# The begin of the Gram stage: the constant row is made first, and two weight loads go behind the second step's transfers

## Chip, cores and metric

The kernel runs on one core of one Trainium2 chip. What counts is the time of one execution in device microseconds (us), as the median of several runs. All data is fp32. The engines are named as the profile names them: PE (TensorE, with its weight loads as PEld), DVE (VectorE), ACT (ScalarE), POOL (GpSimd) and SP (SyncE, which here only issues DMA transfers).

## The reference

Two bottleneck layers run one after the other on `x` of shape (64, 1024, 14, 14). Both have the same form, cut here to what matters:

```python
def layer(x, w1, g1, be1, w2, g2, be2, w3, g3, be3, residual_scale):
    out = relu(bn(conv1x1(x, w1), g1, be1))            # 1024 -> 256
    out = relu(bn(conv3x3(out, w2, pad=1), g2, be2))   # 256 -> 256
    out = bn(conv1x1(out, w3), g3, be3)                # 256 -> 1024
    out = softplus(residual_scale)[0] * out
    return relu(x + out)

def bn(x, gamma, beta):      # statistics of this batch
    mean, var = mean(x, axis=(0, 2, 3)), var(x, axis=(0, 2, 3))
    return gamma * (x - mean) * rsqrt(var + 1e-5) + beta
```

## The kernel before

**Stages.** The 64 x 196 = 12544 pixels (`NPX`) of all images are columns; channels are the 128 partitions (`P`). The 256 middle channels are two halves (`MS`), and all of them stay in SBUF as `y_all` [128, 2, 12544]. Per layer `b` the kernel does the first convolution, the 3x3 convolution (whose last stage is the `columns` matmuls), then a Gram stage, and then the third convolution with the residual sum, which for layer 0 is woven together with layer 1's first convolution.

**What the Gram stage is for.** The third batch norm needs mean and variance of a convolution that has not run yet. As that convolution is linear, both follow from the sums and the products of the 256 middle channels over all pixels. `gram` (line 1116) computes this matrix of products. It works through the pixels in 49 blocks of 256 columns (two groups of 128, `CH` = 2). For each block the channels have to be turned into columns and the pixels into partitions: a tile `zt` [128 pixels, 2, 256 channels + 2 columns of ones]. Six `zt` buffers are used in turn. TensorE then multiplies the block with itself, 8 matmuls for each block, into two accumulators, `upper` in the PSUM bank with the tag `cp` and `lower` in the bank `ap`. While it does so for one block, the next block's `zt` is being made.

**Two ways to make `zt`.** In the order of the code:

- Blocks 0 to 3 and 4 to 7 (the two pieces in `still`) are turned by TensorE: `by_tensor` does four transposes by matmul with the identity (line 1205) into a PSUM tile, and VectorE adds a constant row `c_row` while it copies the result into `zt` (line 1212).
- Blocks 8 to 48 (the seven pieces in `moved`: step 0 has five blocks, steps 1 to 6 have six each) are first rearranged by DMA. `move(k)` sends the 32x32 squares of step k into one of three buffers in turn, `homes[k % 3]`: for step 0 eight transfers of SP and eight of POOL with 80 KB each, for each later step seven of SP and five of POOL with 96 KB. The squares on the diagonal are copied by ScalarE (`stay(k)`). For the first layer one of the three buffers is the tile `ws`. `by_vector` (line 1221) is then a VectorE transpose of 32x32 squares.

Before a block can be used, `y_all` must be normalized in place: scale, shift and relu, by ScalarE (`norm`, recorded at the helper's line 338) or VectorE (`norm_vector`, lines 590 and 592). For accuracy a constant for each channel is subtracted too: on VectorE in place for the moved pieces (`less`, line 1163), and for the others by the `c_row` that is added after the transpose. `c_row` holds that constant as a row, the same in all partitions: `center_row` (line 1191) makes it with two matmuls of `minus_c` against the identity into a PSUM tile with the tag `ax`, and ScalarE copies it to SBUF.

**The order of the begin.** `pairs()` (line 1228) writes it out by hand: norms of the first two blocks, norms of the next two, `center_row`, and then the blocks, with norms, subtractions and moves in between; `n` counts the first eight blocks. `move(0)` is at n = 1, `move(1)` at n = 4, `move(2)` at n = 7, and each later `move` stands two steps ahead of its use. `keep_in_program_order` fixes the order of the instructions that it wraps on their engine; others may be placed by a scheduler, which also assigns the waits. `busy` (line 180) issues filler matmuls, identity against a broadcast column with 448 columns, whose results nobody reads: seven of them into the bank `m` at the end of the 3x3 convolution (line 1106), and one into `ax` after the transposes of block 0. A filler counts as two passes in the trace, as fp32 matmuls do.

**The weights.** The third convolution's weights `w3` (one transfer of 1 MB, `load_w3`, line 168) and, in layer 0, the next layer's `w1` (four transfers of 256 KB, `load_w1`, line 136) are issued on SP ahead of the Gram (lines 1649 and 1651). Their first readers stand near the end of the Gram: `combine_w3` after block 38 and `combine_w1` after block 44 (`beside`), which form weight sums on VectorE.

Of the kernel before, what the change touches and what calls it, by code (L numbers as in the profile page):

```python
# [38 lines left out]
FP = mybir.dt.float32  # L39
# [3 lines left out]
P = 128  # L43
N, C, H, W = 64, 1024, 14, 14
HW = H * W
M = 256
CS = C // P
MS = M // P
# [9 lines left out]
Q = P // 2  # L58
# [32 lines left out]
def bottlenecks(ctx: ExitStack, tc: tile.TileContext, x, w1s, w2s, w3s, pars, out):  # L91
    nc = tc.nc
# [40 lines left out]
            )  # L133
        return xt

    def load_w1(pool, b, queue):

        w = pool.tile([P, MS, 2, CS // 2, P], FP, tag="w1", name=f"w1_{b}")
        n = CS // 2
        for h, o in itertools.product(range(2), range(MS)):  # L140

            step = n // 2 if b == h == o == 0 else n
            for s in range(0, n, step):
                queue.dma_start(out=w[:, o, h, s : s + step], in_=w1s[b][:, o, h, s : s + step])
        return w

    def sums_tile(pool, n):

# [16 lines left out]
        n = CS // 2  # L165
        return combine([[w[:, k, o * n : (o + 1) * n] for k in range(MS)] for o in range(2)], s)

    def load_w3(pool, b):
        w = pool.tile([P, MS, CS, P], FP, tag="w3", name=f"w3_{b}")
        nc.sync.dma_start(out=w, in_=w3s[b])  # L170
        return w

    def matmul(*args, **kw):

        tc.keep_in_program_order(nc.tensor.matmul(*args, **kw))  # L175

    def busy(psum, tag, n, with_=None):

        v = ident if with_ is None else with_
        for i in range(n):  # L180
            matmul(psum.tile(448, tag), v, v[:, :1].to_broadcast([P, 448]), start=True, stop=True)

    def filters(pieces, spare):

# [409 lines left out]
    def conv2(b, par, aff, early, rest):  # L594
# [457 lines left out]
        psum, pool, stats = rest  # L1052
# [12 lines left out]
        l, m, l2 = first.bank("l"), second.bank("m"), second.bank("l")  # L1065
# [22 lines left out]
        queue = queue[1:] + list(itertools.islice(coming, 1))  # L1088
        for k in range(1, NG * NF):
# [13 lines left out]
            item.columns(*qs)  # L1103
            finished.send(item)
            queue = queue[1:] + list(itertools.islice(coming, k > 1))
        busy(psum, "m", 7)

    def conv3(psum, t, o, w3, tag=None):
        ps = psum.tile(tag=tag)
# [3 lines left out]
            )  # L1113
        return ps

    def gram(psum, pool, homes, aff, minus_c, beside):

        upper, lower = psum.tile(3 * Q + 1, "cp"), psum.tile(2 * Q + 2, "ap")  # L1120
        zts = [pool.tile([P, CH, M + 2], FP, tag=f"zt{i}", name=f"zt{i}") for i in range(NZT)]
        for zt in zts:
            nc.gpsimd.memset(zt[:, :, 0 : M + 2 : M + 1], 1.0)
# [32 lines left out]
        def normed(a, e, slots=both):  # L1156
            for s in slots:
                norm(s, y_all[:, s, a:e], aff, act)
# [31 lines left out]

        def center_row():

            ps = psum.tile(M, "ax")
            for s in range(MS):
                matmul(
                    ps[:, s * P : (s + 1) * P], minus_c[:, s : s + 1].to_broadcast([P, P]), ident, start=True, stop=True
                )
            act(c_row, ps, AF.Copy)
# [28 lines left out]

        def pairs():

            for a in 0, px:  # L1230
                norm_vector(1, y_all[:, 1, a : a + px], aff)
                normed(a, a + px, (0,))
            normed(2 * px, 4 * px, (0,))
            center_row()
            rest = [(piece, s) for piece in still for s in range(MS)]
            (second, end), half = still[1], sum(still[1]) // 2
            for n, a in enumerate(a for piece in still for a in range(*piece, px)):
                yield by_tensor(a)
                if n == 0:
                    busy(psum, "ax", 1)  # L1240
                    norm_vector(1, y_all[:, 1, 2 * px : 4 * px], aff)
                    normed(*moved[0])
                elif n == 1:
                    less(*moved[0])
                    move(0)
                    normed(second, end, (0,))
                    normed(second, half, (1,))
                elif n == 3:
                    norm_vector(1, y_all[:, 1, half:end], aff)
                    normed(*moved[1])  # L1250
                elif n == 4:
                    less(*moved[1])
                    move(1)
                    normed(*moved[2])
                elif n == 5:
                    less(*moved[2], both[:1])
                    stay(1)
                elif n == 6:
                    less(*moved[2], both[1:])
                    normed(*moved[3])  # L1260
                elif n == 7:
                    move(2)
                    stay(2)
            for k, (a, e) in enumerate(moved):
                for i in range((e - a) // px):
                    yield by_vector(k, i)
                    if i in (1, 3) and k and k + 2 < len(moved):
                        less(*moved[k + 2], both[i // 2 : i // 2 + 1])
                        if i == 3:
                            move(k + 2)  # L1270
                            if k + 3 < len(moved):
                                normed(*moved[k + 3])
                            stay(k + 2)
                    elif i in (0, 5) and k > 1 and rest:
                        piece, s = rest.pop(0)
                        less(*piece, (s,))
            assert not rest
# [315 lines left out]
    with tc.tile_pool(name="first", bufs=1) as one, tc.tile_pool(  # L1593
        name="first_x", bufs=2
    ) as x_left, ExitStack() as scope:
        xpools = x_right, x_left
        psum = Psum(scope, ["ps"], ps=4, ay=2)
        for i in range(1, 3):
            one.tile([P, CS // 2, PX], FP, tag=f"at{i}", name=f"at{i}")
        w1 = load_w1(one, 0, nc.scalar)  # L1600
        pair = [load_x(x_right, 0, t, CS if t == 0 else 2) for t in range(2)]
        for b in range(2):
            p = keep.tile([P, NPAR], FP, tag=f"par{b}", name=f"par{b}")
            nc.scalar.dma_start(out=p, in_=pars[b][:, :NPAR])
            par.append(p)
        sps = [softplus(p) for p in par]
        nc.scalar.activation(small.tile([P, 1], FP, tag="root", name="root"), sps[1], AF.Sqrt)
        masks.make_identity(nc, ident)
        busy(psum, "ps", 3, ones)
        w1 = combine_w1(w1, sums_tile(one, 1)[:, 0])  # L1610

        border = Border(0, stats1, x_scope)
        for t, xt in enumerate(pair):
            plain_conv1(psum, t, xt, w1[0], par[0], stats1)


        spare = [y_all[:, i, NPX - CS * PX :] for i in range(MS)]
        pieces = list(itertools.product(range(2), range(MS), range(MS)))
        work = filters(pieces, spare)
        total, calls, count = FSTEPS * len(pieces), 6 * (T // 2 - 1 - CS // MS), itertools.count(1)  # L1620

        def beside():
            i = next(count)
            for _ in itertools.islice(work, total * i // calls - total * (i - 1) // calls):
                pass

        def items():
            for t in range(2, T, 2):
                xs = [load_x(xpools[t // 2 % 2], 0, t + i) for i in range(2)]
                yield Conv1(psum, one, xs, (t, t + 1), w1, par[0], stats1, border)  # L1630

        for _ in stream(items(), T // 2 - 1, beside):
            pass

    for b in range(2):
# [9 lines left out]
        with tc.tile_pool(name=f"last_{b}", bufs=1) as one, tc.tile_pool(  # L1645
            name=f"last_x_{b}", bufs=2 if b == 0 else 5
        ) as x_left:
            xpools = (x_right, x_left) if b == 0 else (x_left, x_left)
            w3 = load_w3(one, b)
            if b == 0:  # L1650
                w1 = load_w1(one, b + 1, nc.sync)
            aff = affine(aggregate(stats2, 0), pb, G2, BE2)
            with ExitStack() as scope:
                if b == 0:
                    psum = Psum(scope, ["cy", "ay", "cx", "cy", "ay"], cy=2, ay=2)
                else:
                    psum = Psum(scope, ["cy", "cx"], cy=2, cx=2, cp=2)
                with tc.tile_pool(name=f"gram_{b}", bufs=1) as pool:
                    def x_tile(name, t=0):
                        return xpools[t].tile([P, CS * PX], FP, tag="x", name=name)  # L1660


                    ws = sums_tile(one, 2 - b)
                    homes = [x_tile("home"), x_tile("home") if b else ws.rearrange("p i n -> p (i n)"), x_tile("home", 1)]

                    made_c, made_a = [], []
                    beside = {NPX // (CH * P) - 10: lambda: made_c.append(combine_w3(w3, ws[:, 0]))}
                    if b == 0:
                        beside[NPX // (CH * P) - 4] = lambda: made_a.append(combine_w1(w1, ws[:, 1]))
                    grams = gram(psum, pool, homes, aff, minus_c, beside)  # L1670

                    made = [conv3(psum, 0, 0, w3, "cx" if b else "ay")]
                    mv3 = small.tile([P, CS, nc.vector.BN_AGGR_DIM], FP, tag="mv3", name="mv3")
                    conv3_stats(psum, pool, grams, w3, mv3, ("cy", "cp", "cy", "cp" if b else "cx"), homes[2])
# [59 lines left out]
```

## Time and profile before

Three runs took 1919.19, 1918.64 and 1917.91 us; the median is 1918.64 us.

| profiled execution | |
|---|---|
| its own time | 1919.69 us |
| span of its instructions | 1917.9 us |
| granted TensorE clock (1 is full speed) | 1.000 |
| 583 to 646 us (layer 0's Gram) | PE busy 62.48 of 63.00, DVE 54.84, ACT 45.42, DMA share 0.74, 221 GB/s |
| 1534 to 1598 us (layer 1's Gram) | PE busy 63.06 of 64.00, DVE 52.26, ACT 45.71, DMA share 0.69, 216 GB/s |
| 646 to 1534 us (between them) | PE busy 883.85 of 888.00, DVE 698.57, DMA share 0.52 |

How to read it: the busy time of an engine leaves out the instructions that only issue or wait, and the DMA share is the mean busy share of the 16 DMA engines. In lines of the timeline the first number is the start in us from the span's begin, the second the duration; an entry in square brackets is how long the engine had been idle before the instruction, and the last thing that it waited for. `out<-in` are the program's names of the tiles. In the chain of waits each line is a stretch of the path that ended last, with start and length; "issue" is a time in which the engine waited for nothing that the profile shows.

### The profile page before, as it was taken

Reading aid. Unit: us, or ns where it says so; the run is one execution under the profiler, and the core shown is the slowest. Engines: PE = TensorE matmul, PEld = TensorE weight load, DVE = VectorE, ACT = ScalarE, POOL = GpSimd, SP = SyncE. Lnnn points to the kernel's source line nnn. Section 1 sums busy time; section 2 is a strip of 40 time slices with the busy share of each in tenths; the row PEclk is TensorE's granted clock in tenths of the full one; section 3 lists DMA queues with packets and bytes.
Section 4 is the critical chain, followed back from the end, with each engine's and each line's share of the span. In section 5 each row is a group of like instructions: output and inputs, shape, how many; then the busy total and the mean of one; then the engine's idle time right before and its main releaser. Section 6 shows DMA issues by size and latency. Waiting matters only on the chain.

```text
span 1917.9 us, 28732 instructions
## 1 busy us (share of the span) xinstructions
PE 1901.9 (99%) x10236; PEld 1595.2 (83%) x10236; DVE 1543.6 (80%) x2491; ACT 1086.2 (57%) x2160; POOL 572.0 (30%) x682
## 2 busy tenths in 40 slices
PE   9999999999999999999999999999999999999999
PEld 5555557999998799999999999989999986555555
DVE  5787767999998867677767767789999986888786
ACT  2222214677778255555555555557777692666665
POOL 0111100211204133333434334302121141666664
PEclk9999999999999999999999999999999999999999
DMA  7777644887956534444444444359788466899898
GB/s 286 273 249 278 216 156 154 208 216 207 220 165 172 205 147 169 169 175 183 179 171 168 168 177 177 125 176 219 212 206 225 139 167 254 289 325 348 313 336 304
DMA packets 198527, 408.77 MB, mean 213 GB/s; under 512 B 37104, under 2 KB 175024, under 8 KB 181872
## 3 DMA queue, kind: packets, MB, share of 16 engines
q1 hardware_dynamic: 159712, 321.85, 49.1%
q0 software_dynamic: 33056, 34.03, 8.6%
q10 hardware_dynamic: 5616, 51.06, 6.4%
q8 instruction: 81, 1.33, 0.3%
q14 instruction: 62, 0.51, 0.1%
HBM read 263.75 MB, written 115.34 MB: 198 GB/s over the span
## 4 chain that ended last, share of the span: by engine, by line
PE 92%; DMA 2%; DVE 2%; ACT 2%; POOL 1%; issue 1%; SPq 0%; DVEq 0%; ACTq 0%; POOLq 0%
PE ay L175 17%; PE cy L175 17%; PE columns L175 14%; PE cp L175 11%; PE ap L175 10%; PE m L175 7%; PE l L175 6%; PE cx L175 5%; PE ax L175 4%; PE ps L175 1%; DMA x<-mid 1%; ACT y L338 1%; ACT home L338 1%; DMA home<-y 1%; POOL home L1184 0%
## 5 line engine op out<-in xcount | busy, mean ns | idle before, releaser
L338 ACT ACTIVATE cu<-cy,scale 128x196 f32<-128x196 f32 (+1 forms) x552 | 256.4, 473 | 280.2 <-PE cy L175 274.8
L175 PE MATMUL columns<-v,ub 128*128 128x224 f32 (+1 forms) x1536 | 302.3, 338 | 2.0 <-ACT columns L846 1.1
L338 ACT ACTIVATE x<-x,shift 128x392 f32<-128x392 f32 x452 | 255.0, 613 | 72.8 <-POOL x L530 53.6
L175 PEld LDWEIGHTS columns<-v,ub 128*128 128x128 f32 x1536 | 269.0, 188 | 7.5 <-ACT columns L846 2.2
L504 DVE SCALAR_TENSOR_TENSOR x<-cp,scale,x 128x196 f32<-128x196 f32 (+1 forms) x368 | 178.2, 484 | 98.8 <-PE cp L175 95.8
L175 PE MATMUL cy<-ct,ws 128*128 128x196 f32 (+1 forms) x736 | 221.8, 383 | 1.2 <-ACT cu L338 1.2
L175 PE MATMUL ay<-at,ws 128*128 128x196 f32 (+1 forms) x768 | 212.7, 382 | 0.0
L525 POOL TENSOR_TENSOR x<-x,cu 128x196 f32<-128x196 f32 (+1 forms) x184 | 160.0, 869 | 172.5 <-ACT cu L338 163.8
L530 POOL TENSOR_TENSOR x<-x,cu 128x392 f32<-128x392 f32 x124 | 125.9, 1015 | 191.5 <-DVE x L504 191.5
L175 PEld LDWEIGHTS ay<-at,ws 128*128 128x128 f32 x768 | 139.3, 190 | 34.5
L175 PEld LDWEIGHTS cy<-ct,ws 128*128 128x128 f32 x736 | 133.4, 190 | 36.4 <-ACT cu L338 3.7
L175 PE MATMUL l<-diffs,ub 128*128 128x224 f32 (+1 forms) x768 | 149.6, 337 | 0.3 <-ACT sd L1476 0.3
L551 POOL TENSOR_TENSOR x<-x,cu 128x392 f32<-128x392 f32 x120 | 121.9, 1017 | 87.2 <-DVE x L504 60.4
L175 PE MATMUL m<-sums,ua 128*128 128x224 f32 (+1 forms) x752 | 146.0, 336 | 0.2 <-DVE sums L667 0.2
L338 ACT ACTIVATE au<-ay 128x196 f32<-128x196 f32 (+1 forms) x140 | 53.4, 381 | 152.3 <-PE ay L175 149.6
L175 PEld LDWEIGHTS l<-diffs,ub 128*128 128x128 f32 x768 | 134.6, 189 | 1.4 <-ACT sd L1476 0.6
L504 DVE SCALAR_TENSOR_TENSOR x<-cx,scale,x 128x196 f32<-128x196 f32 (+1 forms) x184 | 89.1, 484 | 56.7 <-PE cx L175 56.7
L175 PEld LDWEIGHTS m<-sums,ua 128*128 128x128 f32 x752 | 131.4, 189 | 1.3 <-DVE sums L667 0.7
L175 PE MATMUL cy<-y,w 128*128 128x196 f32 (+1 forms) x408 | 125.3, 393 | 0.0
L175 PE MATMUL cx<-y,w 128*128 128x196 f32 (+1 forms) x400 | 122.6, 391 | 0.0
L175 PE MATMUL cp<-y,ws 128*128 128x196 f32 (+1 forms) x368 | 113.6, 390 | 1.9 <-DVE x L504 1.9
L175 PE MATMUL cy<-ct,w 128*128 128x196 f32 (+1 forms) x368 | 110.9, 383 | 0.5 <-ACT cu L338 0.5
(238 smaller groups left out, 3909.3 us busy)
## 6 DMA issues: line engine op xcount, KB each, us to landing
x<-in_x SPq DMA_DIRECT2D x62, 1568.0 KB, 6.8
ub<-u SPq DMA_DIRECT2D x92, 768.0 KB, 5.6
x<-mid SPq DMA_DIRECT2D x32, 1568.0 KB, 8.4
mid<-x ACTq DMA_DIRECT2D x31, 1568.0 KB, 5.1
out<-x SPq DMA_DIRECT2D x123, 392.0 KB, 5.7
ua<-u SPq DMA_DIRECT2D x92, 256.0 KB, 3.1
u<-y POOLq DMA_DIRECT2D x48, 256.0 KB, 5.5
home<-y SPq DMA_DIRECT2D x70, 96.0 KB, 3.6
```

The costliest lines, as they stand in the source:

```text
L175: tc.keep_in_program_order(nc.tensor.matmul(*args, **kw))
L338: tc.keep_in_program_order(nc.scalar.activation(*args, **kw))
L504: nc.vector.scalar_tensor_tensor(v, bank, self.scale[:, o : o + 1], v, ALU.mult, ALU.add)
L525: nc.gpsimd.tensor_add(self.part(1, 1), self.part(1, 1), u3)
L530: nc.gpsimd.tensor_add(v, v, self.u12)
L551: nc.gpsimd.tensor_add(v, v, self.u12[:, i * self.n : (i + 1) * self.n])
```

## The change

- `center_row` moves from behind the first norms to the head of `pairs()`. Its PSUM tile is no longer one of its own with the tag `ax`; it is the unused rest of an accumulator's bank, `cp` in layer 0 and `ap` in layer 1. Its ScalarE copy so stands ahead of the norms in ScalarE's order.
- The seven fillers into `m` at the end of the 3x3 convolution go. Behind the row's matmuls there are five (into the bank `ap` in layer 0, `ax` in layer 1) and one more into `ax`.
- The loads of `w3` and `w1` no longer stand ahead of the Gram. The tiles are allocated there, and `load()` issues the transfers, still on SP, at n = 4: behind SP's seven transfers of `move(1)` and ahead of `move(2)`. Their order is now fixed by hand. The first `w1` of the kernel, loaded at its begin on ScalarE's queue, keeps its place.
- The pool of the Gram stage gets `reuse_waits="tile"`, so that an allocation waits tile by tile for what held its memory before.

In the built programs nothing else moves: VectorE's and POOL's orders are the same.

```diff
-    def load_w1(pool, b, queue):
+    def w1_tile(pool, b):
+        return pool.tile([P, MS, 2, CS // 2, P], FP, tag="w1", name=f"w1_{b}")
+    def load_w1(w, b, queue):
...
-                queue.dma_start(out=w[:, o, h, s : s + step], in_=w1s[b][:, o, h, s : s + step])
-        return w
+                tc.keep_in_program_order(
+                    queue.dma_start(out=w[:, o, h, s : s + step], in_=w1s[b][:, o, h, s : s + step])
+                )
...
-            matmul(psum.tile(448, tag), v, v[:, :1].to_broadcast([P, 448]), start=True, stop=True)
+            matmul(psum.tile(448, tag) if isinstance(tag, str) else tag, v, v[:, :1].to_broadcast([P, 448]), start=True, stop=True)
...
             finished.send(item)
             queue = queue[1:] + list(itertools.islice(coming, k > 1))
-        busy(psum, "m", 7)
...
-        upper, lower = psum.tile(3 * Q + 1, "cp"), psum.tile(2 * Q + 2, "ap")
+        banks = psum.tile(512, "cp"), psum.tile(512, "ap")
+        upper, lower = banks[0][:, : 3 * Q + 1], banks[1][:, : 2 * Q + 2]
...
         def center_row():
-            ps = psum.tile(M, "ax")
+            ps = banks[b][:, M : 2 * M]
...
         def pairs():
+            center_row()
+            busy(psum, "ax" if b else banks[1][:, :448], 5)
+            busy(psum, "ax", 1)
             for a in 0, px:
                 norm_vector(1, y_all[:, 1, a : a + px], aff)
                 normed(a, a + px, (0,))
             normed(2 * px, 4 * px, (0,))
-            center_row()
...
                 elif n == 4:
                     less(*moved[1])
                     move(1)
+                    load()
                     normed(*moved[2])
...
-            w3 = load_w3(one, b)
+            w3 = w3_tile(one, b)
             if b == 0:
-                w1 = load_w1(one, b + 1, nc.sync)
+                w1 = w1_tile(one, b + 1)
...
-                with tc.tile_pool(name=f"gram_{b}", bufs=1) as pool:
+                with tc.tile_pool(name=f"gram_{b}", bufs=1, reuse_waits="tile") as pool:
...
+                    def load():
+                        tc.keep_in_program_order(nc.sync.dma_start(out=w3, in_=w3s[b]))
+                        if b == 0:
+                            load_w1(w1, b + 1, nc.sync)
+                    grams = gram(psum, pool, homes, aff, minus_c, b, load, beside)
```

More of the change, by code (lines that the diff above doesn't have):

```diff
@@ L134, in load_x @@
         return xt
-    def load_w1(pool, b, queue):
-        w = pool.tile([P, MS, 2, CS // 2, P], FP, tag="w1", name=f"w1_{b}")
+    def w1_tile(pool, b):
+        return pool.tile([P, MS, 2, CS // 2, P], FP, tag="w1", name=f"w1_{b}")
+    def load_w1(w, b, queue):
         n = CS // 2
@@ L166, in combine_w3, with w3_tile @@
         return combine([[w[:, k, o * n : (o + 1) * n] for k in range(MS)] for o in range(2)], s)
[L168 to L171, printed above, removed]
+    def w3_tile(pool, b):
+        return pool.tile([P, MS, CS, P], FP, tag="w3", name=f"w3_{b}")
     def matmul(*args, **kw):
@@ L1114, in conv3, with gram @@
         return ps
-    def gram(psum, pool, homes, aff, minus_c, beside):
-        upper, lower = psum.tile(3 * Q + 1, "cp"), psum.tile(2 * Q + 2, "ap")
+    def gram(psum, pool, homes, aff, minus_c, b, load, beside):
+        banks = psum.tile(512, "cp"), psum.tile(512, "ap")
+        upper, lower = banks[0][:, : 3 * Q + 1], banks[1][:, : 2 * Q + 2]
         zts = [pool.tile([P, CH, M + 2], FP, tag=f"zt{i}", name=f"zt{i}") for i in range(NZT)]
@@ L1599, in bottlenecks @@
             one.tile([P, CS // 2, PX], FP, tag=f"at{i}", name=f"at{i}")
-        w1 = load_w1(one, 0, nc.scalar)
+        w1 = w1_tile(one, 0)
+        load_w1(w1, 0, nc.scalar)
         pair = [load_x(x_right, 0, t, CS if t == 0 else 2) for t in range(2)]
@@ L1669, in bottlenecks @@
                         beside[NPX // (CH * P) - 4] = lambda: made_a.append(combine_w1(w1, ws[:, 1]))
-                    grams = gram(psum, pool, homes, aff, minus_c, beside)
+                    def load():
[3 more added lines that the diff above has]
+                    grams = gram(psum, pool, homes, aff, minus_c, b, load, beside)
                     made = [conv3(psum, 0, 0, w3, "cx" if b else "ay")]
```

## The prediction

> **What bounds the kernel now.** I read the page first, then the chain of waits around the two Grams (583 to 646 us and 1534 to 1598 us), then the timelines there, then the DMA windows.
>
> ```profile
> span 1917.9 us, 28732 instructions
> PE 1901.9 (99%) x10236; PEld 1595.2 (83%) x10236; DVE 1543.6 (80%) x2491; ACT 1086.2 (57%) x2160; POOL 572.0 (30%) x682
> ...
> PE 92%; DMA 2%; DVE 2%; ACT 2%; POOL 1%; issue 1%; SPq 0%; DVEq 0%; ACTq 0%; POOLq 0%
> ```
>
> TensorE sets the time: 99% busy, 92% of the chain. All that is left beside its work is 1917.9 - 1901.9 = 16 us of idle, so a change that removes no useful matmul can win only pieces of that. One piece stands at the begin of each Gram (chain of waits, start and length in us):
>
> ```profile
> 579.44 5.29 PE m L175 x14
> 584.73 0.37 PE ax L175 x4
> 585.10 0.19 ACT y L338
> 585.29 0.42 issue
> 585.71 0.37 ACT c_row L338
> 586.08 0.04 issue
> 586.12 1.02 PE ax L175 x2
> ```
>
> Seven filler matmuls (14 passes), then the constant row's two, then the chain leaves TensorE for 1.0 us: it goes over ScalarE's copy of `c_row`. The timeline says why:
>
> ```profile
> 584.01 1.80 ACT L338 ACTIVATE y<-y,shift,scale 128x256 f32<-128x256 f32 x3 [1.14 <-DVE shift L1508]
> ...
> 585.01 0.60 PE L1205 MATMUL cy<-ident,y 128*128 128x128 f32 x4
> ...
> 586.12 1.02 PE L175 MATMUL ax<-ident 128*128 128x448 f32 x2 [0.52 <-ACT c_row L338]
> 586.16 0.69 DVE L1212 TENSOR_TENSOR zt<-cy,c_row 128x512 f32<-128x512 f32 x1 [0.63 <-ACT c_row L338]
> ```
>
> The copy is queued behind three norms, though its input needs none of them. TensorE waits for it 0.52 us (its next filler reuses the bank that the copy reads), VectorE 0.63. The second Gram shows the same at 1537.59 (0.51) and 1537.62 (0.63).
>
> The second part of the change moves weights on SP's queue:
>
> ```profile
> 579.87 0.35 SPq L170 DMA_DIRECT2D w<-in_w  x1
> 580.27 2.08 SPq L144 DMA_DIRECT2D w<-in_w  x4
> 590.00 5.52 SPq L1184 DMA_DIRECT2D home<-y  x8
> 595.77 5.05 SPq L1184 DMA_DIRECT2D ws<-y  x7
> 600.93 12.74 SPq L1184 DMA_DIRECT2D home<-y  x14
> ```
>
> Now the weights go out ten microseconds ahead of `move(0)` (590.00) and have landed by 587.9; nothing waits for them until the combinations on VectorE at 631.75. Where they go, the queue is close packed. What they would meet there is visible where VectorE waits for transfers, and in the DMA share (last but one column; before it length, then busy us of PE, PEld, DVE, ACT and POOL, and the clock):
>
> ```profile
> 604.15 1.31 DVE L1221 STREAM_TRANSPOSE zt<-ws 128x512 f32<-128x512 f32 x2 [1.33 <-DMA ws<-y]
> ...
> 617.21 0.71 DVE L1221 STREAM_TRANSPOSE zt<-home 128x512 f32<-128x512 f32 x1 [0.76 <-DMA home<-y]
> ```
>
> ```profile
> 606.00:608.00 2.00, 2.00 (x34) 1.82 (x32) 2.00 (x4) 1.97 (x2) 0.00 (x0) 1.00 0.41 95
> 608.00:610.00 2.00, 2.00 (x34) 1.79 (x32) 2.00 (x4) 2.00 (x3) 1.18 (x3) 1.00 0.33 76
> ```
>
> **The row ahead of the norms.** In the built order `center_row` stands right behind the last `columns` matmul; its wait is for a VectorE result from before 576, so it starts at 579.3. Then come 5 + 1 fillers instead of 7. Row 0.44 us (584.57 to 585.01) plus 12 passes of 0.378 (5.29 / 14) gives 579.28 + 0.44 + 4.54 = 584.26: TensorE is ready 0.75 us earlier than at 585.01, and idles until the norms. ScalarE's copy (0.36) falls into its wait of 1.14 us before 584.01, between `sd` (ends 582.87) and the first norm: hidden at no cost, and if that cover were gone the norms would be 0.27 later (585.71 to 585.98). The transposes need ScalarE's first norm (584.01 + 0.60 = 584.61) and VectorE's first pair (584.58 + 0.29 = 584.87). I add 0.08 for the handover, so the second transpose starts at 584.95; three of them (0.45) bring the filler to 585.40 instead of 586.12: **0.72 us** gained. Bounds: 0.52 (only the wait goes) and 0.75. VectorE's first sum can start at 585.5 instead of 586.16, behind its second norm pair (ends 585.53): 0.66. The dropped filler (0.76) is worth nothing by itself; TensorE waits for norms in its place.
>
> Does the lead last through blocks 0 to 12? I took, block by block, the time between the end of VectorE's `zt` and TensorE's first weight load on it: 0.17 us at block 7, 0.23 at block 8, else 0.35 or more. These `zt` move with TensorE's transposes and with `less`, whose norms on ScalarE come 0.27 earlier with slack behind them; `move(0)` goes at 589.4. So the lead holds to within 0.05. The pool's waits by tile release memsets that already stand behind POOL's statistics (until 581.4): nothing.
>
> **The weights, first Gram.** `load()` stands behind `move(1)`'s seven SP transfers and ahead of `move(2)`'s. SP issues w3 at 600.93 - 0.72 + 0.1 = 600.3, w1's four pieces until 602.8 (0.35 + 2.08 and gaps), then `move(2)`: 2.5 - 0.72 = 1.8 us later than now. SP allows eight transfers in flight: in the built order each waits for the landing of the one eight places before. So the fourth to seventh transfer of `move(2)` now wait for w3 and for three pieces of w1. POOL's five of `move(2)` and of `move(3)` are queued elsewhere but use the same engines.
>
> The 2.1 MB took 5.0 us of all DMA engines (share 0.84 of 582 to 588). Behind `move(1)` (lands 604.0 - 0.7 = 603.3) and beside POOL's half until 605, I put w3's landing at 606.5, the pieces of w1 0.63 apart, the third at 608.4; the last transfer of `move(2)` then takes 0.6 for its issue and 2.2 (the shortest landing of the group): **611.2** instead of 608.9 now. Below: 609.8, if the idle share around 606 to 610 takes most of it. Above: 613.2, all 5.0 us added to 608.2.
>
> The Trainium skill (DMA: Bandwidth & Descriptors, "Issuing engines are not separate DMA queues") says that transfers of all issuers end on the same 16 engines and interleave; taken alone it speaks against this change and gives the 613.2, which would make the sum about 2 us worse. The windows above show 0.59 x 2 + 0.67 x 2 = 2.5 us of engine time free in 606 to 610; 613.2 - 2.5 = 610.7 is near my value.
>
> What is late next? VectorE transposes `move(2)`'s first block now at 609.60, long after the landing, and `move(3)`'s at 617.21 after 0.76 of waiting; 617.21 - 0.76 - 609.60 = 6.85 us is its own work between, in order, `less` for later steps included. In that stretch TensorE's smallest margin is 0.82 (block 27). With TensorE 0.72 earlier 0.10 is left, so the first block has to start by 617.31 - 6.85 = 610.46. It starts at 611.2 + 0.15: 0.9 late, and TensorE gives that back. First Gram: -0.72 + 0.9 = **+0.2** (bounds -0.72 and +2.2).
>
> **The weights, second Gram.** Only w3, one transfer. Here VectorE is the tight engine:
>
> ```profile
> 1556.91 1.30 DVE L1221 STREAM_TRANSPOSE zt<-home 128x512 f32<-128x512 f32 x2 [2.96 <-DMA home<-y]
> ```
>
> From there it runs without a pause to 1581.4, TensorE's margins being 0.05 to 0.15 at blocks 13 to 17, and TensorE waits 0.43 at 1587.94. So the end moves with `move(1)`'s landing, which is ahead of w3 and follows `less`: 0.72 earlier. `move(2)` lands at 1559.89 now; 2.5 us more (half of 5.0) and 0.72 less is 1561.7, and VectorE wants it at 1562.37 - 0.72 = 1561.65: 0.1 late. Second Gram: **-0.6** (bounds -0.72 and +0.9, the latter if POOL's half is pushed too and 1.5 more is lost).
>
> **Sum.** +0.2 - 0.6 = -0.4 on a span of 1917.9, that is 1917.5. That execution took 1919.69 in all, 1.8 around its span, and the runs' median is 1918.64; I take the difference off the median: **1918.2**.
>
> **The rivals.**
> A. All hidden: the idle DMA time takes the weights and both Grams keep their lead. For it: 2.5 us free right there, VectorE 2.5 us ahead of TensorE at block 19 (ends 610.27, used 612.73). Against it: eight in flight, and VectorE's order. -1.44: 1917.2. Chance 0.27.
> B. Slower: the transfers of `move(2)` become the bound. It decides from a landing after 612.0, when the first Gram's loss (612.0 + 0.15 - 610.46 - 0.72 = 1.0) outweighs the gain in the second. For it: DMA share 0.83 to 0.96 in 602 to 606, and VectorE's in-order delay that carries into `move(4)`. At 613.2: +2.2 - 0.5 = +1.7, 1920.3. If the weights only got the profile page's mean of 213 GB/s, they would need 9.8 us instead of 5.0: 4.8 and 2.4 more on top, about +7, 1926. Chance 0.25.
> C. The row doesn't leave the path, because TensorE waits for the new banks at 579: then about nothing is won, 1919. Against it: the results awaited are three microseconds old. Chance 0.03.
>
> **The numbers.** The forecast holds 0.45, with its own range 1917.6 to 1919.0. The range adds A's whole gain and half the runs' spread (0.6) below, 1916.6, and above the upper bounds of both Grams together, +2.2 + 0.9 = +3.1, which is B with POOL's half pushed in the second Gram too: 1921.7. A change of 0.2% (3.8 us, what a measurement here can tell from none) is out of reach for the gain: at most 1.5 of 16 us idle; 0.03 for what the layout of all the code may do. Slower by that much needs B's bad end, beyond both upper bounds: 0.12, half of B. Same: 0.85.
>
> **What would show it.** Right: the copy of `c_row` before 583.5, TensorE's first `ax` filler behind the transposes near 585.4 without a wait on `c_row`, blocks 0 to 12 about 0.7 earlier against the end of `columns`. For the weights: w issues near 600.3, the last of `move(2)` landing near 611, and a VectorE wait on `home` at the first block of step 2 that was not there. Wrong: no such wait (A), or TensorE idle of over 1 us before a `zt` around 612 to 620 (B); or a wait at 579 (C).

## The result and the profile after

Six runs of the changed kernel took 1930.09 to 1934.22 us, median 1931.43; six of the kernel before 1917.91 to 1920.60, median 1919.09. The ratio is 1.0065 with an interval of 1.0054 to 1.0076: **12.3 us slower**, where the prediction said 1918.2 with a range up to 1921.7.

From the page of the profiled execution (1932.31 us in all, against 1919.69 before):

```profile
span 1930.5 us, 28733 instructions
PE 1905.5 (99%) x10232; PEld 1598.9 (83%) x10232; DVE 1544.1 (80%) x2491; ACT 1087.2 (56%) x2160; POOL 571.1 (30%) x682
```

TensorE's idle time is now 1930.5 - 1905.5 = 25.0 us instead of 16, and its busy time is 3.6 us longer (1905.5 - 1901.9). TensorE's list of waits (total us, times, longest) names the place. The wait for `zt` before, and then the first two lines after:

```profile
PE cp L175 <- DVE zt L1221: 0.4, 1, 0.4
```

```profile
PE cp L176 <- DVE zt L1222: 10.8, 4, 6.6
PE cy L176 <- ACT cu L339: 1.7, 4, 0.5
```

To see where time is lost, I took for each block of a Gram the time from the end of the last `columns` matmul to TensorE's first weight load on that block's `zt`, after minus before:

```
block             0      7      8     18     19     21     48
first Gram    -0.91  -0.91  +0.07   0.00  +6.87  +8.48  +8.44 us
second Gram   +0.08  +0.07  +0.07  +0.08  +3.23  +4.52  +4.77 us
```

Block 19 is the first of step 2, whose transfers stand right behind the weights. The chain of waits of the changed kernel runs through just that:

```profile
600.74 0.66 SPq L1677
...
601.44 0.84 SPq L147
...
602.32 0.64 SPq L147
...
603.00 9.28 DMA w<-in_w
...
612.30 6.58 DMA home<-y
...
619.11 0.72 DVE zt L1222
...
619.88 0.91 PE cp L176 x4
```

SP issues the weights until 604.5; the third piece of `w1` lands 9.28 us after its issue; only then does the last transfer of `move(2)`, eight places behind it, go out (612.30), and it takes 6.58 us more, where the same transfer took 2.2 before. VectorE starts block 19 at 619.11; before it was at 609.60:

```profile
609.60 0.67 DVE L1221 STREAM_TRANSPOSE zt<-home 128x512 f32<-128x512 f32 x1
```

The entry of the first Gram, on the other hand, came much as forecast (timeline; start and length in us):

```profile
579.55 0.61 PE L176 MATMUL cp<-ident,minus_c 128*128 128x128 f32 x4
...
583.03 0.36 ACT L339 ACTIVATE c_row<-cp 128x256 f32<-128x256 f32 x1
...
584.93 0.83 PE L1206 MATMUL cy<-ident,y 128*128 128x128 f32 x4 [0.23 <-ACT y L339]
...
585.59 0.92 PE L176 MATMUL ax<-ident 128*128 128x448 f32 x2
585.89 0.69 DVE L1213 TENSOR_TENSOR zt<-cy,c_row 128x512 f32<-128x512 f32 x1
```

The copy of `c_row` is done long before the sum needs it, and neither TensorE nor VectorE waits for it.

### The profile page after: what moved, and what is told of

Its sections match the earlier page's. It is cut to its first block, busy times and chain, and to the rows that moved or that the text cites. A ratio compares the mean times of both kernels' runs of the same rounds, so it can differ in the third digit from the quotient of the medians.

```text
span 1930.5 us, 28733 instructions
## 1 busy us (share of the span) xinstructions
PE 1905.5 (99%) x10232; PEld 1598.9 (83%) x10232; DVE 1544.1 (80%) x2491; ACT 1087.2 (56%) x2160; POOL 571.1 (30%) x682
## 4 chain that ended last, share of the span: by engine, by line
PE 85%; issue 5%; DVE 3%; DMA 3%; ACT 1%; POOL 1%; SPq 1%; DVEq 0%; POOLq 0%; ACTq 0%
PE cy L176 17%; PE ay L176 14%; PE columns L176 13%; PE cp L176 10%; PE ap L176 8%; PE m L176 6%; PE l L176 6%; PE cx L176 5%; PE ax L176 4%; DMA home<-y 1%; PE ps L176 1%; SPq L1185 1%; POOL u L223 1%; DMA w<-in_w 0%; DVE zt L1222 0%
## 5 line engine op out<-in xcount | busy, mean ns | idle before, releaser
L176 PE MATMUL cp<-zt 128*64 128x193 f32 x784 | 102.3, 335 | 10.8 <-DVE zt L1222 10.8
```

## The experiments

The theory: the bytes of the weights, put ahead of `move(2)`, are the whole loss, by the time of the DMA engines. The first rival: the row part costs. The second: not the bytes but the five places in SP's queue, as each of SP's transfers waits for the landing of the one eight places before. A ratio is to the kernel before, with its interval.

### Each part alone

Row part alone: `load()` is empty and the transfers stand at their old place.

```diff
             w3 = w3_tile(one, b)
+            nc.sync.dma_start(out=w3, in_=w3s[b])
             if b == 0:
                 w1 = w1_tile(one, b + 1)
+                load_w1(w1, b + 1, nc.sync)
...
                     def load():
-                        tc.keep_in_program_order(nc.sync.dma_start(out=w3, in_=w3s[b]))
-                        if b == 0:
-                            load_w1(w1, b + 1, nc.sync)
+                        pass
```

> The row part of the change alone; the weights go out ahead of the Gram as before. Theory (the weights' DMA time behind move(1) is the whole loss): 1917.8 to 1919.6 us; TensorE starts the first Gram's block 0 about 0.9 us earlier against the end of columns, most of that is given back at block 8 (move(0) lands no earlier), and in the second Gram nothing is won, because there each filler waits for the one before it (1.08 us for each pair of passes instead of 0.76). No TensorE wait before block 19, clock 1.000. Rival (the row part itself costs: banks, fillers, waits of the pool): 1925 or more, with TensorE waiting in blocks 0 to 18.

Measured: 1920.36 us, ratio 1.0008 (1.0000 to 1.0017). Block 0 of the first Gram is 0.91 us earlier, block 8 0.27 later, block 0 of the second 0.08 later. There were four waits for `zt` of 2.1 us in all, none over 0.9, two of them before block 19, where none was expected. The time lies above its expected range, and the interval begins at 1.0000: the row part alone won nothing that can be measured, and it costs far too little to be the loss.

Weights' part alone: `center_row`, the seven fillers in `m` and the pool as before, `load()` as in the change.

```diff
+        busy(psum, "m", 7)
...
-            center_row()
-            busy(psum, "ax" if b else banks[1][:, :448], 5)
-            busy(psum, "ax", 1)
...
             normed(2 * px, 4 * px, (0,))
+            center_row()
```

> The weights' part alone: the row, the seven fillers and the pool are as before. Theory: nearly all of the loss, 1929 to 1933 us, with TensorE waiting about 6 us before block 19 in the first Gram and about 3 us in the second, and its clock at 0.5 for some us behind both. Rival (the row part, or both together, make the loss): under 1924.

Measured: 1930.67 us, ratio 1.0066 (1.0052 to 1.0080), which can't be told from the changed kernel. Its TensorE waits:

```profile
PE cp L176 <- DVE zt L1222: 8.5, 5, 6.2
```

So the weights' part is the loss, and the first rival falls. The second Gram's wait was shorter than expected, 0.8 us before block 19 instead of 3 (block 19 came 1.1 us later).

### The fillers of the second Gram

In the second Gram the row's gain is missing from the first block on. There `busy(psum, "ax", n)` takes a new tile of a tag with one buffer for every filler, and each waits for the one before; in the first Gram five of the six write a slice that is taken once. The next run is the row part alone (the weights ahead of the Gram, as above) with one tile for all six:

```diff
-            busy(psum, "ax" if b else banks[1][:, :448], 5)
-            busy(psum, "ax", 1)
+            ax = psum.tile(448, "ax")
+            busy(psum, ax if b else banks[1][:, :448], 5)
+            busy(psum, ax, 1)
```

> The row part alone, and the six fillers write one tile of the bank ax that is taken once, so that none waits for the one before it. Theory: the second Gram's entry is about 1.0 us shorter than with the row part alone and the fillers stand 0.38 us apart for each pass, 1916.8 to 1918.6 us in all. Rival (the second Gram's entry is held by ScalarE's norms and not by the fillers): within 0.3 us of the row part alone.

Measured: 1918.10 us, ratio 0.9998 (0.9989 to 1.0006). The timeline of the changed kernel, and then of this run:

```profile
1540.03 6.31 PE L176 MATMUL ax<-ident 128*128 128x448 f32 x12
1546.18 0.60 PE L1206 MATMUL cy<-ident,y 128*128 128x128 f32 x4
```

```profile
1530.78 4.70 PE L176 MATMUL ax<-ident 128*128 128x448 f32 x12
1535.72 0.82 PE L1206 MATMUL cy<-ident,y 128*128 128x128 f32 x4 [0.24 <-ACT y L339]
```

The same twelve passes take 1.6 us less, and block 0 of the second Gram comes 0.91 us earlier than before instead of 0.08 later. That is shown in the trace; in the time of the whole kernel this version can't be told from the kernel before. It was the fastest tried, and none was faster beyond its interval.

### Bytes or places

The same five transfers at the changed place, but with 8 of 128 partitions; the other 120 go ahead of the Gram.

```diff
+            nc.sync.dma_start(out=w3[8:], in_=w3s[b][8:])
...
-                        tc.keep_in_program_order(nc.sync.dma_start(out=w3, in_=w3s[b]))
+                        tc.keep_in_program_order(nc.sync.dma_start(out=w3[:8], in_=w3s[b][:8]))
                         if b == 0:
-                            load_w1(w1, b + 1, nc.sync)
+                            load_w1(w1, b + 1, nc.sync, slice(0, 8))
```

> As the changed kernel, but 120 of the 128 partitions of each weight transfer go ahead of the Gram; the same five transfers (one in the second Gram) at the changed place carry only the other 8 partitions, 128 KB instead of 2.1 MB. Theory (engine time of the bytes): the last transfer of move(2) lands before 611 us, at most 1 us of wait before block 19, 1918 to 1921 us. Rival (five places in SP's queue, and eight transfers in flight, so that move(2) waits for the landing of the weights): the transfers of move(2) still go out 2.5 us later and wait for the slivers' landing, 4 us or more of wait before block 19, 1924 us or more.

Measured: 1919.44 us, ratio 1.0004 (0.9995 to 1.0012). VectorE's first transposes of step 2 (timeline) in the changed kernel and in this run:

```profile
619.11 0.71 DVE L1222 STREAM_TRANSPOSE zt<-home 128x512 f32<-128x512 f32 x1 [8.49 <-DMA home<-y]
```

```profile
610.84 0.71 DVE L1222 STREAM_TRANSPOSE zt<-home 128x512 f32<-128x512 f32 x1 [0.35 <-PE ap L176]
```

VectorE no longer waits for a transfer there. Places with next to no bytes cost no time in this kernel. They do put the row off: SP issues the last transfer of `move(2)` about 4 us later than with the row part alone (608.13 instead of 604.00), but block 19 isn't wanted so soon. Two more sizes, with `w1` ahead of the Gram: all of `w3` late, and one half of `w3` late.

```diff
                 w1 = w1_tile(one, b + 1)
+                load_w1(w1, b + 1, nc.sync)
...
-                        if b == 0:
-                            load_w1(w1, b + 1, nc.sync)
```

> As the changed kernel, but in the first Gram only w3 (1 MB, one transfer) goes at the changed place; the four pieces of w1 (1 MB) go ahead of the Gram. Theory (the price is the DMA engines' time for the bytes, in a row of transfers without spare time): the first Gram then loses what the second does in the changed kernel, about 4.5 us with the lower clock behind the wait in place of 8.5, so 1927.4 us, 1926 to 1929. Rival (the one big transfer is the cause, the small pieces are absorbed): 1930 or more.

```diff
             w3 = w3_tile(one, b)
+            nc.sync.dma_start(out=w3[:, 0], in_=w3s[b][:, 0])
             if b == 0:
                 w1 = w1_tile(one, b + 1)
+                load_w1(w1, b + 1, nc.sync)
...
-                        tc.keep_in_program_order(nc.sync.dma_start(out=w3, in_=w3s[b]))
-                        if b == 0:
-                            load_w1(w1, b + 1, nc.sync)
+                        tc.keep_in_program_order(nc.sync.dma_start(out=w3[:, 1], in_=w3s[b][:, 1]))
```

> As the changed kernel, but in both Grams only one half of w3 (512 KB, one transfer) goes at the changed place, the rest ahead of the Gram. Theory: a quarter of the first Gram's bytes and half of the second's; the wait before block 19 is 0 to 1.5 us in each, and no fall of the clock follows, as the wait is short: 1920 to 1923 us. Rival (a fixed price of a large transfer in the row): 1926 or more.

Measured: 1923.22 us, 1.0023 (1.0014 to 1.0032), and 1919.24 us, 1.0000 (0.9991 to 1.0009). Both were cheaper than expected. With 1 MB the first Gram loses 0.4 us before block 19, not the 3 of the second Gram: up to there it has time to spare. With 0.5 MB nothing is lost before block 19 in either Gram (the second lost 1.1 us between blocks 21 and 40, which I didn't follow up).

### With bytes, the places count

If bytes alone set the landing, one transfer of 1 MB for `w1` should change nothing:

```diff
-                            load_w1(w1, b + 1, nc.sync)
+                            tc.keep_in_program_order(nc.sync.dma_start(out=w1, in_=w1s[b + 1]))
```

> As the changed kernel, but w1 goes as one transfer of 1 MB instead of four pieces: the same bytes at the same place in two places of SP's queue instead of five, so that only the sixth and seventh transfer of move(2) wait for a landing of the weights. Theory (the landing of move(2) is put off by 5 to 6 us for each MB ahead of it, whatever the number of transfers): the last of move(2) lands 11 us later than with the row part alone, 1930 to 1933 us. Rival (with bytes, the wait eight places back is what lets POOL's move(3) pass move(2)): it lands 2 us or more sooner than in the changed kernel, 1927 to 1929.5 us.

Measured: 1929.20 us, 1.0058 (1.0042 to 1.0075). The last of `move(2)` lands at 614.99 instead of 618.89, and the wait before block 19 is 3.7 instead of 6.6 us. The landing comes 3.9 us sooner, as the rival of this run had it; in this program only the seventh transfer of `move(2)` has a weight transfer eight places ahead (`w3`, landed at 608.03). The whole time decides less: the four runs took 1927.16 to 1931.18 us, across both expectations, and the interval overlaps that of the changed kernel. And the rows of `w1`'s transfers had changed too, from 2 KB to 8 KB. So the same bytes again as four transfers, with rows of 8 KB:

```diff
-                            load_w1(w1, b + 1, nc.sync)
+                            for i in range(4):
+                                here = slice(32 * i, 32 * i + 32)
+                                tc.keep_in_program_order(nc.sync.dma_start(out=w1[here], in_=w1s[b + 1][here]))
```

> As the changed kernel, but w1's four transfers of 256 KB are cut by partitions (32 rows of 8 KB each) and not by columns (128 rows of 2 KB each): five places in SP's queue as in the changed kernel, rows of 8 KB as in the run with two transfers. If the five places are what put off the last of move(2) from 615.0 (two transfers) to 618.9 us (changed kernel): it lands near 618 to 619, behind POOL's move(3), with 6 to 7 us of wait before block 19, 1930 to 1933 us. If the length of the rows is: near 615, 3.5 to 4.5 us of wait, 1927 to 1930 us.

Measured: 1931.75 us, 1.0069 (1.0052 to 1.0086); landing at 618.00, wait 6.3 us. So it is the places and not the length of the rows. Three issues of this run show how (timeline): the third piece of `w1`, POOL's five of `move(3)`, and SP's last transfer of `move(2)`.

```profile
601.77 0.48 SPq L1681 DMA_DIRECT2D w<-in_w  x1
...
609.63 2.74 POOL L1185 DMA_DIRECT2D home<-y  x5 [8.12 <-DVE y L1164]
...
612.16 0.58 SPq L1185 DMA_DIRECT2D home<-y  x1
```

The third piece of `w1` lands at 612.14, and 0.02 us later SP issues the last transfer of `move(2)`, eight places behind it. Meanwhile POOL, whose order has no weights in it, has issued its five of `move(3)`, and they land by 617.8, ahead of that last one. With two transfers the last of `move(2)` goes out at 608.05 and lands ahead of all five.

All landings of SP's last transfer of `move(2)` in the first Gram, from the end of `columns`:

```
kernel                      late in SP's queue        landed    wait before block 19
row part alone              nothing                   28.35 us  none
half of w3 late             0.5 MB, one transfer      30.86     none
w3 late                     1 MB, one transfer        33.13     0.2 us
w1 in one transfer          2 MB, two transfers       35.91     3.7
w1 by rows                  2 MB, five transfers      38.75     6.3
changed kernel              2 MB, five transfers      39.18     6.6
```

Each is one execution. They give about 5 us for the first MB, 3 for the second, and 3 more for the five places. Some 4.4 us behind the landing of the row part alone are free (33.13 - 28.35, less the 0.4 that block 19 came late): block 19 isn't wanted sooner.

The 3 us for the places are the least certain of these sizes. Five transfers at the changed place were also in the weights' part alone and in the run with fillers below, and their landings were 39.57 and 37.90; two transfers stand in one execution only. In the second Gram, where the same single transfer is late in six of the kernels, the landing varies from 32.79 to 35.42. That the order of landing changes is shown; how much time it costs isn't known to better than that.

### Other places

One move later, behind `move(2)`:

```diff
                     move(1)
-                    load()
...
                     move(2)
+                    load()
                     stay(2)
```

> As the changed kernel, but load() stands one move later, behind move(2)'s transfers and ahead of move(3)'s. Theory (5 to 6 us of delay for each MB for what stands behind it, idle DMA time taking little of it): move(3) lands some 8 to 11 us late before block 25, where VectorE had no time to spare, 1928 to 1933 us. Rival (the DMA engines' idle share of 606 to 617 us in the kernel before, 4.6 us, takes most of the weights, as the prediction's sum had it): 1 to 3 us of wait, 1920 to 1923 us.

Measured: 1926.72 us, 1.0043 (1.0028 to 1.0058): between the two expectations. The first Gram loses nothing at block 19 and 3.8 us at block 25 (a wait of 3.5 us), and 1.7 us more by block 31, while the granted clock was 0.50 from 623.8 to 627.2 us; the second loses 1.1 us. Against the end of `columns`, the last of SP's `move(3)` lands 4.9 us later than with the row part alone (42.56 instead of 37.70). The same five transfers with the same bytes put `move(2)` off by 10.8 us (39.18 - 28.35): what a load costs hangs on its place, not on its bytes alone.

Behind the last move, where no transfer of the Gram follows:

```diff
                     move(1)
-                    load()
...
                             move(k + 2)
+                            if k + 3 == len(moved):
+                                load()
```

> As the changed kernel, but load() stands behind SP's transfers of the last step, move(6), so that no transfer of the Gram is behind it; the same five transfers and bytes. Theory (it's the place ahead of other transfers that costs, not the weights' coming late): no wait before block 19, 1918 to 1922 us, as the row part alone or up to 2 us more if combine_w3 has to wait for w3. Rival (any load inside the Gram takes the moves' DMA time): 1926 or more.

Measured: 1936.28 us, 1.0085 (1.0072 to 1.0099), the slowest. The number lies in the rival's range, but neither account holds: no move was put off, and nothing was lost before block 21. Then came this, on the chain of waits and on VectorE:

```profile
634.04 4.94 DMA w<-in_w
```

```profile
639.08 0.69 DVE L158 TENSOR_TENSOR ws<-w 128x512 f32<-128x512 f32 x1 [7.53 <-DMA w<-in_w]
```

`move(6)` can't go out until its buffer is free (628.5 to 634.0), so `w3` lands at 639.0, and `combine_w3` stands in VectorE's order ahead of the last blocks' transposes. The weights were late for their own reader, and the transposes waited behind it.

### What the lower clock costs

Fillers between block 18's matmuls and block 19's, in the changed kernel:

```diff
+            if k == 19:
+                busy(psum, psum.tile(448, "ax"), 3 if b else 8)
             before = zt
```

> As the changed kernel, with filler matmuls behind block 18's matmuls and ahead of block 19's, eight in the first Gram (6.1 us) and three in the second (2.3 us), so that TensorE isn't idle while it waits. Theory (the waits before block 19 cost twice: the wait itself, and 1.6 and 1.3 us of half clock behind it): the waits stay, the granted clock stays at 1.0, and 2.9 us are won: 1928.5 us, 1927.5 to 1929.5. Rival (the slow blocks 19 to 21 are held by VectorE and not by the clock): 1931 to 1932, as the changed kernel.

Measured: 1928.22 us, 1.0045 (1.0032 to 1.0057), 3.2 us less than the changed kernel. The timeline of the changed kernel, and then of this run:

```profile
619.88 0.91 PE L176 MATMUL cp<-zt 128*64 128x193 f32 x4 [6.58 <-DVE zt L1222]
620.58 0.65 PE L176 MATMUL ap<-zt 128*64 128x129 f32 x4
...
623.79 0.50 PE L176 MATMUL cp<-zt 128*64 128x193 f32 x4
624.11 0.40 PE L176 MATMUL ap<-zt 128*64 128x129 f32 x4
```

```profile
612.85 6.31 PE L176 MATMUL ax<-ident 128*128 128x448 f32 x16
619.09 0.55 PE L176 MATMUL cp<-zt 128*64 128x193 f32 x4
619.47 0.39 PE L176 MATMUL ap<-zt 128*64 128x129 f32 x4
```

After 6.6 us of idling the same four matmuls take 0.91 and 0.65 us; behind fillers they start at 0.55 and 0.39. In this run block 21 is no later than block 19 (+6.30 and +6.36); in the changed kernel it lost 1.61 us more. The granted clock of this run's whole span was 1.000. Not all of the 3.2 us need be the clock, as block 19 itself came 0.5 us sooner here (+6.36 against +6.87 us). The 1.6 and 1.3 us that the changed kernel lost between blocks 19 and 21 also fit the 3.6 us by which TensorE's busy time grew.

## Why the prediction was wrong, point by point

**The step that failed** is "I put w3's landing at 606.5 [...] the last transfer of `move(2)` then takes 0.6 for its issue and 2.2 [...]: 611.2 [...] Above: 613.2, all 5.0 us added to 608.2". It landed at 618.9. The forecast had `w3` at 606.5, the third piece of `w1` at 608.4, and 2.8 us from there to the last landing; measured were 609.21, 612.29 and 6.6 us. Three things were wrong in it.

- The weights' price. The 5.0 us were to be the DMA engines' time for the weights when little else ran, and the forecast let 3.0 of them show (611.2 - 608.2). The figure was itself too small: the weights went out from 579.87 on, and the window taken begins at 582. Before (last columns: clock, DMA share, GB/s):

```profile
580.00:582.00 2.00, 2.00 (x7) 1.03 (x6) 2.00 (x6) 0.00 (x0) 1.73 (x15) 1.00 0.45 98
```

  With that window it is 0.45 x 2 + 5.0 = 5.9 us, and the bytes of both together are the whole 2.1 MB. The windows (last columns: clock, DMA share, GB/s) of the row part alone, and then of the changed kernel:

```profile
602.00:606.00 4.00, 4.00 (x64) 3.78 (x61) 2.71 (x5) 3.91 (x6) 0.00 (x0) 1.00 0.89 260
606.00:610.00 4.00, 4.00 (x62) 3.83 (x60) 4.00 (x7) 3.98 (x4) 1.34 (x3) 1.00 0.13 28
```

```profile
602.00:606.00 4.00, 4.00 (x63) 3.76 (x61) 2.25 (x5) 3.94 (x5) 0.00 (x0) 1.00 0.99 309
606.00:610.00 4.00, 4.00 (x63) 3.80 (x61) 4.00 (x7) 3.97 (x4) 0.30 (x1) 1.00 1.02 318
610.00:614.00 4.00, 3.30 (x49) 2.95 (x44) 0.62 (x2) 3.90 (x5) 2.38 (x5) 1.00 1.09 197
614.00:618.00 4.00, 0.00 (x0) 0.00 (x0) 0.00 (x0) 2.56 (x2) 0.00 (x0) 0.81 0.99 213
```

  The idle time was there (0.13 in 606 to 610, more than I had counted), and the weights filled it; but the engines then stayed full to 618. And it was time behind the row: with the row part alone the last of `move(2)` had landed at 607.24. So most of it could not be taken off the delay of `move(2)`, as the prediction did with its 2.5 us. With few places the weights put the landing off by 35.91 - 28.35 = 7.6 us, not by 3.0, and with five by 10.8. Rival B's "if the weights only got the profile page's mean of 213 GB/s, they would need 9.8 us" was nearer to that; I had it and left it out of the range. Why it is 7.6 and not the 5.9 of the weights' own engine time stays open.
- The upper bound was no bound. Adding the weights' own engine time leaves out what passes the waiting transfers. I had seen that the fourth to seventh transfer of `move(2)` wait for weights, and that POOL's of `move(3)` are queued elsewhere, but gave the second no price. It is about 3 us (35.91 to 38.75 and 39.18), by one execution each.
- What a long wait does to the matmuls behind it: 1.6 and 1.3 us of lower clock, in no term of the sum.

**Rival B** was the case that came true, with its place and its sign; its price of +1.7 was far too small. It said that TensorE idle of over 1 us before a `zt` at 612 to 620 would show it, and that is the wait of 6.6 us.

**The weights, second Gram.** Forecast -0.6; +4.8 measured. The landing of `move(2)` had been put 1.8 us later; against the end of `columns` it came 6.2 us later (1574.98 - 1539.74 = 35.2 instead of 1559.89 - 1530.90 = 29.0). Both are of one execution. In the six profiled kernels with all of `w3` late here, the second Gram lost from 2.2 to 5.2 us, so the sign is sure and the size is not.

**The row ahead of the norms** was right in mechanism in the first Gram, and nearly in size: 0.72 forecast, 0.91 at block 0 (above its own bound of 0.75), the copy at 583.03 (I had said before 583.5), the filler behind the transposes at 585.59, which is 585.32 when the 0.27 us are taken off by which this execution reached the end of `columns` later.

**"So the lead holds to within 0.05"** failed at block 8, where +0.07 stands instead of -0.91. Block 8's `zt` waits for the last transfer of `move(0)`, and that didn't land earlier (599.78 against 599.53, or 20.1 us from the end of `columns` in both). I had listed its margin of 0.23 us as one that moves with the norms, but it hangs on transfers. The row part alone lost its lead at the same place, so it isn't lost to the weights alone; the weights' part alone, which has no lead to lose, had block 8 come 0.83 us later. Why `move(0)` took longer to land stays open; block 8 came between 0.37 us earlier and 0.49 later than before in the runs with the row part.

**The second Gram's entry** was forecast like the first's, and gained nothing. I had costed six fillers at 0.378 us for each pass and missed that in the second Gram each takes a new tile of one buffer. That was to be read in the diff: `"ax" if b else banks[1][:, :448]`.

**Rival C and the chances.** TensorE didn't wait at 579. "Slower by over 0.2%" had 0.12 and was what came.

## What to carry to other kernels

A load that is moved into a row of close transfers is to be priced at what the row leaves it, not at its speed when alone, and whatever stands behind it in its queue is late by that plus what other queues send ahead meanwhile. If a queue allows a fixed number of transfers in flight, follow each transfer behind the moved ones to the landing that it waits for. And a load that hides at no cost where it is has nothing to win elsewhere: here only the row part could have given anything, and what it won at the begin of the first Gram was gone at block 8.

## What the runs showed of the hardware

- **The clock falls within a short wait.** These windows (clock in the last column but two) are of the changed kernel's second Gram, where TensorE idles 2.87 us from 1573.40:

```profile
1574.00:1575.00 1.00, 0.00 (x0) 0.00 (x0) 0.00 (x0) 1.00 (x1) 0.00 (x0) 1.00 0.63 189
1575.00:1576.00 1.00, 0.00 (x0) 0.00 (x0) 0.50 (x1) 1.00 (x2) 0.00 (x0) 0.82 0.24 74
1576.00:1577.00 1.00, 0.73 (x6) 0.56 (x8) 1.00 (x3) 0.88 (x1) 0.00 (x0) 0.50 0.71 175
```

  A mean of 0.82 between 1.00 and 0.50 puts the fall at 1575.6, 2.2 us after the last matmul. In the first Gram it came 3.2 us after, by the same reckoning (0.62 in 616 to 618). The Trainium skill (TensorE: Matmul & The Clock Gate, "What's actually happening") says that the clock is halved after at least one idle window of about 3.4 us, and that the window is free-running, so that the point of a change varies. The half rate and the shift from case to case agree; falls 2.2 and 3.2 us after the last matmul are sooner than its figure, and the second Gram's whole wait of 2.87 us is shorter than it. At the same place, waits of 1.84 us (`w1` in one transfer) and 1.51 us (`w1` by rows) left the clock at 1.00, and one of 3.16 us (`w3` late) was followed by 0.50.
- **A DMA share over 1.** Between 610 and 614 the share is 1.09 at 197 GB/s, while the weights alone moved at 425 GB/s before, at a share of 1.03 (582 to 584). The packets' times overlap there, so the share says that the engines are full, not how much they move.
